# A convolution-and-attention kernel on one core: the second layer's matmuls in another order, and wide tiles for the relative logits' transposes

## The chip, the core and the metric

The kernel runs on one NeuronCore of a Trainium2 chip. The core has five engines that run side by side and meet at semaphores: TensorE (PE, matmuls and transposes; its weight loads are listed apart as PEld), VectorE (DVE), ScalarE (ACT), GpSimd (POOL) and SyncE (SP, which only issues DMAs here). The metric is the time of one execution on the device in microseconds. The kernel before the change took 2448.43 us, the median of three runs (2446.56 to 2452.04).

## The reference

Eight images of 32x32 pixels and 256 channels go through two layers, all in fp32. Cut to what matters:

```python
x = x + L0_conv(_gn(x), ...)                    # layer 0: 3x3 convolution (192 channels) beside
                                                # 8-head attention with relative logits (64 channels)
t = _to_tokens(x)                               # 1024 tokens an image
t = t + L1_attn(_ln_t(t), W_q, W_k, W_v, W_o, b_o)
t = t + L1_ffn(_ln_t(t), Wr, br, W1, b1, W2, b2, gamma, beta)   # two of eight experts an image

def L1_attn(inputs, W_q, W_k, W_v, W_o, b_o):   # U = 128
    Q, K, V = inputs @ W_q, inputs @ W_k, inputs @ W_v
    w = softmax(Q @ K.T / sqrt(U))
    return (w @ V) @ W_o + b_o + inputs

def L0_attention:                               # 8 heads of 8 channels
    logits = q @ k.T + rel_w + rel_h            # relative logits of row and column
    weights = softmax(logits)
```

The change lies in the second layer's attention (`L1_attn`) and in the work of the next image's first layer that is threaded through it.

## The kernel before, in words

One program handles the images one after the other, and then the expert layer for all of them. Within the loop over images the order of TensorE's instructions is the order in the text (`manual_schedule` for PE); the orders on VectorE, ScalarE and GpSimd are set by the framework's scheduler. So work of the next image is woven in by hand, as Python generators that are advanced a step at a time.

Image b goes through these stages:

- `conv_layer_attention` (L675 on): first-layer attention, in steps s. A step takes two score products of one head and 128 rows (`score`, L583) with a maximum on VectorE (L591), two groups of exponentials (`weigh`, L623 and L631) and their products with the values (`gather`, L640); the first 10 steps have scores alone. Products of the image's convolution that are still to do are spread over those 10 steps: `first` of them ahead of the first step, then `todo` in each.
- Near its end `ahead()` normalises the next image, and `more()` starts that image's `input_steps` (keys, queries, values).
- `attention_layer` (L758 on): layer norm, transposes of the normalised tokens (`tpn`, L779), query and key projections (`pq`, L795), value projection (`pv1`, L811), then a loop over eight tiles of 128 queries: `scores(i)` (L832, maximum L841, exponential L843), `turn(i)` (eight transposes of the weights, L852, copied out half by VectorE, L855, half by ScalarE, L857), and for every two tiles `gather(ib)` (sixteen products with the values, L863, copied out by ScalarE as `os`, L867) and `project(ib, os)` (output projection L875, then VectorE's additions L879 and statistics L880).
- Meanwhile `fill(us)` advances the next image's `input_steps`. Each step yields a length in us and a number of convolution products, which `fill` then runs (`conv.run`). The steps are: relative logits (`prel`, L468, 32-column products, copied out at L480 and L482), eight steps of them, then the transposes of the width logits (`tpw`, L493, copied into `rwq` at L495 and L497), four steps of four transposes. After the last, `Unit(0, ...)` is made, whose constructor issues the loads of the next image's first unit on SP (L555, L559, L566).

A convolution (`conv_steps`, L501 on) has 72 products (L515) in six groups of twelve; a group accumulates in one bank of PSUM and is copied out by ScalarE (L524), and GpSimd adds it to the image. The image's first 36 products run in `more` and `fill`, before its own turn, in the bank of the pool `po`, which is the only one; `conv.whole()` finishes an open group. The others run in the pool `st`.

The PSUM pools: `lg`, two tiles of two banks (scores, `prel`); `st`, three tiles of one bank (`tpn`, `tpw`, `pq`, `pv1`, `tp`, `pa1`); `po`, one tile of one bank. A tile asked for when none is free makes its first writer wait for the reader of an older one.

Of the kernel before, what the change touches and what calls it, by code (L numbers as in the profile page):

```python
# [20 lines left out]
NT = S // P  # L21
# [15 lines left out]
def kernel(  # L37
# [54 lines left out]
    with ExitStack() as ph:  # L92
# [27 lines left out]
        def st_tile(name):  # L120
            return ps_st.tile([P, 512], FP, tag="st", name=name)
# [263 lines left out]
        def input_steps(b, held):  # L385
# [69 lines left out]
            for which in range(2):  # L455
                for half in range(2):
                    prs = lg_tile("prel")
                    for i in range(16):
                        a = half * 16 + i
                        for g in range(NG):  # L460
                            rows = slice(DK + 32 * g, DK + 32 * g + 32)
                            dst = prs[:, g, i * 32 : (i + 1) * 32]
                            if which == 0:
                                table, mov, m = half_w, kqv[rows, :, a], WW - 1 - a
                            else:
                                table, mov, m = half_h, kqv[rows, a, :], HH - 1 - a
                            for k in range(2):
                                nc.tensor.matmul(  # L468
                                    dst[64 * k : 64 * k + 64], lhsT=table(rows, m, k), rhs=mov, start=True, stop=True
                                )  # L470
                        if i == 7:
                            yield 1.4, 4 - which * half
                    for g in range(NG):
                        if which == 0:
                            dst = rw[g].rearrange("p (x y) -> p y x", y=WW)[:, half * 16 : half * 16 + 16, :]
                            src = prs[:, g, :].rearrange("p (y x) -> p y x", x=HH)
                        else:
                            dst, src = rh[g][:, half * 512 : (half + 1) * 512], prs[:, g, :]
                        if g == 0:
                            nc.vector.tensor_copy(dst, src)  # L480
                        else:
                            nc.scalar.copy(dst, src)  # L482
                    if which == 0 and half == 1:
                        for g in range(NG):
                            nc.sync.dma_start(out=rwd[g], in_=rw[g])
                    yield 1.4, 4 - which * half

            for t2 in range(NT // 2):
                tp = st_tile("tpw").rearrange("p (t g c) -> p t g c", t=2, g=NG)
                for i in range(2):  # L490
                    t = t2 * 2 + i
                    for g in range(NG):
                        nc.tensor.transpose(tp[:, i, g, :], rw[g][:, t * P : (t + 1) * P], ident)  # L493
                if t2 % 2:
                    nc.vector.tensor_copy(rwq[:, t2 * 2 : t2 * 2 + 2], tp)  # L495
                else:
                    nc.scalar.copy(rwq[:, t2 * 2 : t2 * 2 + 2], tp)  # L497
                yield 0.43, 0
            held["units"] = [Unit(0, kq, rh, rwd)]

        def conv_steps(b, place):  # L501
# [179 lines left out]
        def conv_layer_attention(b, units, kq, rh, rwd, rwq, conv, early, ahead, more):  # L681
# [6 lines left out]
            units.append(Unit(1, kq, rh, rwd))  # L688
            left = conv.left
            lead = NT + LAG  # L690
            first = min(left, 3 * KC)
            conv.run(first)
            left -= first
            for s in range(NU * NT + lead + 2):
# [60 lines left out]
            more(0, 4)  # L755


        def attention_layer(b, fill, whole):  # L758

# [20 lines left out]
                for kc in range(KC):  # L782
                    nc.scalar.copy(nT[:, kc, q * 512 : (q + 1) * 512], tps[kc].rearrange("p j t -> p (j t)"))
            nc.gpsimd.tensor_tensor(T[b], T[b], bo.to_broadcast([P, NT, C]), ALU.add)
            fill(5.6)
            whole()

            qkv = f_tile("qkv").rearrange("p a e s -> p (a e s)")
            qk = [qkv[:, i * S : (i + 1) * S] for i in range(2)]
# [1 line left out]
            for i in range(2):  # L791
                for q in range(2):
# [10 lines left out]
                        nc.vector.tensor_copy(qk[i][:, q * 512 : (q + 1) * 512], pq)  # L803
                    else:
                        nc.scalar.copy(qk[i][:, q * 512 : (q + 1) * 512], pq)
            for q in range(2):
                pv = st_tile("pv1").rearrange("p (j u) -> p j u", u=U)
                for j in range(4):
                    t = q * 4 + j
# [70 lines left out]
                    nc.vector.bn_stats(st2[:, t, :], tt)  # L880
                    nc.vector.bn_aggr(mv2[:, b, t, :], st2[:, t : t + 1, :])

            for i in range(NT + 1):
                if i < NT:
                    scores(i)
                ib, odd = divmod(i - 3, NIB)
                os = None
                if ib >= 0 and not odd:
                    os = gather(ib)
                elif i:  # L890
                    fill(0.8)
                if i:
                    turn(i - 1)
                if os is not None:
                    project(ib, os)
            fill(1.0)
            for ib in range(max(0, (NT - 2) // NIB), NT // NIB):
                os = gather(ib)
                fill(0.8)
                project(ib, os)  # L900


            m = mv2[:, b]
# [33 lines left out]
        class Conv:  # L937
# [13 lines left out]
            def whole(self):  # L951

                self.run(self.left % (6 * KC))
# [17 lines left out]
        with tc.manual_schedule(engines={mybir.EngineType.PE}):  # L971
            conv = Conv(0)
            means = []
            for b in range(B):
# [36 lines left out]
                def fill(us):  # L1011

                    while us > 0:
                        took, products = next(steps, (None, None))
                        if took is None:
                            break
                        us -= took
                        conv.run(products)

                means.append((b, *attention_layer(b, fill, conv.whole)))  # L1020
                fill(1000.0)
                del T[b]
            token_mean(*means.pop())

# [282 lines left out]
```

## Time and profile before

| | |
|---|---|
| median of three runs | 2448.43 us |
| the profiled execution, its own time | 2444.67 us |
| its span, first to last instruction | 2442.9 us |
| mean granted TensorE clock | 0.981 |
| scores of the second layer (L832) | 119.1 us busy in 256 records |
| its value products (L863) | 116.6 us in 512 |
| convolution products (L515) | 236.1 us in 1152 |
| transposes `tpw` (L493) | 19.6 us in 128 |

A line of the profile names the source line, the engine, the operation, the tile written and the tile read, and their shapes. `x8` means that eight instructions in a row are merged. In brackets stands how long the engine had been idle and what it waited for. An image takes some 239 to 240 us, from one first score of its second layer to the next. The expert layer is the last 443 us of the span.

### The profile page before, as it was taken

To read this page: it belongs to the slowest core of one execution; us is meant where nothing else is said; L and a number is where in the kernel's file an instruction comes from. 1 tells how busy PE (TensorE), PEld (TensorE's weight loads), DVE (VectorE), ACT (ScalarE), POOL (GpSimd) and SP (SyncE) were. 2 spreads that over 40 slices of the span, in tenths; PEclk is the share of its full clock that TensorE was granted. 3 is DMA by queue.
4 is the path that set the end of the run, shared out by engine and by line. 5 is a ranking of instruction groups with operands and counts; after the bars stand their busy time and mean duration, and the time that the engine had idled before them with its cause. 6 is when DMAs were issued, how large, how long until landed. Compare 5 with 4: busy or idle time off the path is not lost. (4 is left out here: it accounts for less than half of the span.)

```text
span 2442.9 us, 41840 instructions
## 1 busy us (share of the span) xinstructions
PE 2314.1 (95%) x17273; PEld 1299.7 (53%) x17273; DVE 1485.5 (61%) x2661; ACT 1026.1 (42%) x1717; POOL 475.6 (19%) x446
## 2 busy tenths in 40 slices
PE   5999999999999999999999999999998879999998
PEld 4535643564366436643663376337632546666665
DVE  7776487548755875587467746774774434444443
ACT  2255336433643464346335732563266323222232
POOL 3202130213031202210230023002301032222221
PEclk7999999999999999999999999999999989999999
DMA  4521242134222412240324032403240032121210
GB/s 124 82 40 27 41 97 39 35 46 90 32 43 57 80 22 51 57 85 9 58 70 72 4 57 70 72 4 57 60 66 2 23 121 69 69 69 69 70 60 26
DMA packets 71468, 135.82 MB, mean 56 GB/s; under 512 B 12000, under 2 KB 24168, under 8 KB 69232
## 3 DMA queue, kind: packets, MB, share of 16 engines
q1 hardware_dynamic: 65488, 115.47, 23.7%
q0 software_dynamic: 3056, 15.73, 1.9%
q8 instruction: 136, 2.23, 0.4%
q10 hardware_dynamic: 2736, 1.97, 0.3%
q14 instruction: 52, 0.43, 0.1%
HBM read 53.43 MB, written 25.17 MB: 32 GB/s over the span
## 5 line engine op out<-in xcount | busy, mean ns | idle before, releaser
L591 DVE TENSOR_REDUCE my<-lg 128x32 f32<-128x1024 f32 x512 | 618.5, 1223 | 161.8 <-PE st L623 125.9
L631 ACT ACTIVATE PT<-st 128x512 f32<-128x512 f32 (+1 forms) x944 | 541.6, 633 | 306.2 <-PE st L623 301.7
L623 PE MATMUL st<-F,km 32*128 32x512 f32 x2048 | 545.2, 641 | 17.2 <-DMA F<-mb 11.9
L583 PE MATMUL lg<-km,F 24*128 24x512 f32 x2048 | 534.9, 637 | 6.1 <-DMA F<-kq 3.7
L640 PE MATMUL po<-PT,vall 128*32 128x256 f32 (+1 forms) x3200 | 315.1, 453 | 2.9 <-ACT PT L631 2.4
L583 PEld LDWEIGHTS lg<-km,F 24*128 24x128 f32 x2048 | 156.0, 183 | 186.5 <-issue 112.1
L515 PE MATMUL pc<-convw,gdif 128*128 128x192 f32 x1152 | 236.1, 345 | 11.5 <-ACT m L524 8.7
L640 PEld LDWEIGHTS po<-PT,vall 128*32 128x32 f32 x3200 | 66.9, 108 | 314.6 <-issue 280.1
L515 PEld LDWEIGHTS pc<-convw,gdif 128*128 128x128 f32 x1152 | 186.8, 192 | 81.5 <-issue 59.9
L623 PEld LDWEIGHTS st<-F,km 32*128 32x128 f32 x2048 | 177.5, 184 | 96.3 <-issue 43.5
L1220 PE MATMUL phd<-n2T,w 128*128 128x512 f32 x512 | 223.7, 594 | 0.0
L1237 PE MATMUL py<-w,hT 128*128 128x256 f32 x1024 | 223.6, 379 | 0.0
L1237 PEld LDWEIGHTS py<-w,hT 128*128 128x128 f32 x1024 | 194.6, 190 | 33.3 <-issue 7.4
L311 POOL TENSOR_TENSOR T<-T,l0b 128x2048 f32<-128x2048 f32 x8 | 36.4, 4546 | 633.5 <-PE tpx L304 633.5
L1220 PEld LDWEIGHTS phd<-n2T,w 128*128 128x128 f32 x512 | 97.0, 191 | 114.9 <-issue 107.7
L1244 DVE TENSOR_TENSOR r<-py,n 128x256 f32<-128x256 f32 x64 | 27.1, 423 | 215.0 <-PE py L1237 215.0
L863 PE MATMUL po<-pt,qkv 128*128 128x256 f32 x512 | 116.6, 381 | 11.3 <-DVE pt L855 11.3
L524 ACT COPY m<-pc 128x384 f32<-128x384 f32 x48 | 23.0, 479 | 247.3 <-PE pc L515 247.3
L1227 ACT ACTIVATE hT<-phd,b1c 128x512 f32<-128x512 f32 x128 | 86.3, 686 | 96.5 <-PE phd L1220 96.3
L841 DVE TENSOR_REDUCE nm<-lg 128x1 f32<-128x1024 f32 x64 | 78.1, 1220 | 77.5 <-PE lg L832 77.5
L780 POOL TENSOR_TENSOR T<-T,n 128x256 f32<-128x256 f32 x64 | 47.1, 743 | 372.8 <-DVE n L775 372.8
L832 PE MATMUL lg<-qkv 128*128 128x512 f32 x256 | 119.1, 593 | 0.0
(250 smaller groups left out, 2627.6 us busy)
## 6 DMA issues: line engine op xcount, KB each, us to landing
F<-rh SPq DMA_DIRECT2D x256, 128.0 KB
F<-kq SPq DMA_DIRECT2D x256, 64.0 KB
F<-rwd SPq DMA_DIRECT2D x256, 64.0 KB
w<-in_L_ffn_W_dram SPq DMA_DIRECT2D x32, 512.0 KB
rwd<-rw SPq DMA_DIRECT2D x16, 512.0 KB
Td<-T POOLq DMA_DIRECT2D x8, 1024.0 KB, 8.3
T<-Td SPq DMA_DIRECT2D x8, 1024.0 KB
out_dram<-yo SPq DMA_DIRECT2D x16, 512.0 KB
```

Source lines behind the costliest of these rows:

```text
L515: nc.tensor.matmul(pc[:, v, :], lhsT=gflat[:, 2 * pair + v, kc, at : at + P], rhs=convw[:, 2 * pair + v, dy, kc * CO : (kc + 1) * CO], sta ...
L583: nc.tensor.matmul(lg[:, a, :], lhsT=self.F[r : r + 24, a, 0, i * P : (i + 1) * P], rhs=KM[self.g][r : r + 24, a].rearrange("p e k -> p (e ...
L591: nc.vector.tensor_reduce(my[:, :, hl], lg.rearrange("p a (y x) -> p y a x", y=WW), AX.XY, ALU.max)
L623: nc.tensor.matmul(st[:, i, :] if len(heads) > 1 else st, lhsT=KM[self.g][r : r + 32, a, e, :], rhs=self.F[r : r + 32, a, e, :], start=Tru ...
L631: nc.scalar.activation(self.pts[j][:, hs, :], st, AF.Exp)
L640: nc.tensor.matmul(self.po[32 * hl : 32 * hl + 32, cols], lhsT=vall[:, j, h * (DH + 1) : h * (DH + 1) + 32], rhs=self.pts[j][:, hl, cols], ...
L832: nc.tensor.matmul(lg[:, h, :], lhsT=qk[0][:, i * P : (i + 1) * P], rhs=qk[1][:, h * 512 : (h + 1) * 512], start=True, stop=True,)
L841: nc.vector.tensor_reduce(nm, lg, AX.X, ALU.max, negate=True)
L863: nc.tensor.matmul(po[:, 0:IB], lhsT=v1[:, jc, :], rhs=pt[:, jc, :], start=jc == 0, stop=jc == NT - 1)
L1220: nc.tensor.matmul(phd, lhsT=ws[k][0][:, kc, f * P : (f + 1) * P], rhs=n2T[:, kc, q * 512 : (q + 1) * 512], start=kc == 0, stop=kc == KC - 1,)
L1227: nc.scalar.activation(hT[:, k * NF + f, :], phd, AF.Gelu, bias=b1c[:, f, k * B + b : k * B + b + 1])
L1237: nc.tensor.matmul(py, lhsT=hT[:, k * NF + f, j * P : (j + 1) * P], rhs=ws[k][1][:, f, :], start=k == 0 and f == 0, stop=k == TOPK - 1 and ...
```

## The change

Five things are changed, all in the order of work or in the tiles used; the arithmetic is the same.

```diff
@@ input_steps: products per step, and wide transposes
-                            yield 1.4, 4 - which * half
+                            yield 1.4, 4 - (which == half == 0)
...
-                    yield 1.4, 4 - which * half
+                    yield 1.4, 4 - (which == half == 0)
-            for t2 in range(NT // 2):
-                tp = st_tile("tpw").rearrange("p (t g c) -> p t g c", t=2, g=NG)
-                for i in range(2):
-                    t = t2 * 2 + i
+            for t4 in range(2):
+                tp = lg_tile("tpw").rearrange("p q (t g c) -> p (q t) g c", t=2, g=NG)
+                for i in range(4):
+                    t = t4 * 4 + i
                     for g in range(NG):
                         nc.tensor.transpose(tp[:, i, g, :], rw[g][:, t * P : (t + 1) * P], ident)
...
-                yield 0.43, 0
+                yield 0.86, 0
@@ conv_layer_attention
-            first = min(left, 3 * KC)
+            first = left % (3 * lead)
@@ attention_layer (now given the Conv object, not its method whole)
-            fill(5.6)
-            whole()
+            fill(1000.0)
+            conv.whole()
...
-            for q in range(2):
+
+            def values(q):
                 pv = st_tile("pv1").rearrange("p (j u) -> p j u", u=U)
...
-            for i in range(NT + 1):
-                if i < NT:
-                    scores(i)
+            for i in range(NT):
+                scores(i)
+                if i < 2:
+                    values(i)
                 ib, odd = divmod(i - 3, NIB)
-                os = None
                 if ib >= 0 and not odd:
                     os = gather(ib)
-                elif i:
-                    fill(0.8)
                 if i:
                     turn(i - 1)
-                if os is not None:
+                if ib >= 0 and not odd and i + 1 < NT:
                     project(ib, os)
-            fill(1.0)
-            for ib in range(max(0, (NT - 2) // NIB), NT // NIB):
-                os = gather(ib)
-                fill(0.8)
-                project(ib, os)
+            turn(NT - 1)
+            project(NT // NIB - 2, os)
+            os = gather(NT // NIB - 1)
+            conv.place[0] = st_tile
+            conv.run(2)
+            project(NT // NIB - 1, os)
@@ the loop over images
-                means.append((b, *attention_layer(b, fill, conv.whole)))
-                fill(1000.0)
+                means.append((b, *attention_layer(b, fill, conv)))
```

- The value projection, sixteen products, ran as a block behind the query and key projections. Now its first half stands behind the scores of tile 0 and its second half behind those of tile 1.
- The end of the layer ran as: gather 2, transposes of tile 6, projection 2, transposes of tile 7, gather 3, projection 3. Now it is: gather 2, transposes of tile 6, transposes of tile 7, projection 2, gather 3, two convolution products of the next image (in an `st` bank), projection 3.
- The convolution products of the eight steps of relative logits were 4, 4, 4, 4, 4, 4, 3, 3, and are 3, 3, 4, 4, 4, 4, 4, 4. The sum stays 30; with 4 in `more` and 2 in the step ahead it is 36.
- `first`, the products ahead of an image's first scores, was 6, and is what is left over when 30 is taken out: 4 of 34 for all images but the first (30 then go in tens of three), and 12 of 72 for the first (then six a step, where it had six steps of seven and four of six).
- The transposes of the width logits go eight to a `lg` tile of two banks, in two steps, where they went four to an `st` tile of one bank, in four; so there are two copies of 1024 elements (one on ScalarE, one on VectorE) for four of 512.

## The prediction

> **What bounds the kernel now.** I read the page first: TensorE (PE) is busy 95% of the span, no other engine more than 61%.
>
> ```profile
> span 2442.9 us, 41840 instructions
> PE 2314.1 (95%) x17273; PEld 1299.7 (53%) x17273; DVE 1485.5 (61%) x2661; ACT 1026.1 (42%) x1717; POOL 475.6 (19%) x446
> ```
>
> An average can hide stages with another limit, so next the stretches of one image (the second; columns: length, then busy time of each engine, granted clock, DMA share, GB/s).
>
> ```profile
> 454.00:494.00 40.00, 37.17 (x685) 31.54 (x684) 15.92 (x39) 12.45 (x22) 17.10 (x18) 1.00 0.36 67
> 508.00:541.00 33.00, 30.98 (x150) 23.09 (x151) 19.78 (x44) 14.67 (x27) 0.00 (x0) 1.00 0.02 5
> 548.00:579.00 31.00, 30.51 (x154) 16.16 (x150) 28.51 (x38) 3.12 (x7) 19.98 (x25) 1.00 0.44 107
> ```
>
> The first two, which the change rewrites, are PE's: VectorE is under 60% busy, ScalarE under 45%. The third, the first scores of the next image, is VectorE's (28.51 of 31). A microsecond saved on PE ahead of it counts only if VectorE can start earlier too.
>
> Third, the list of waits on PE alone: who was waited for, us in total, times, longest.
>
> ```profile
> PE po L863 <- DVE pt L855: 11.3, 8, 1.4
> PE pc L515 <- ACT m L524: 8.7, 14, 0.6
> PE tp L852 <- ACT pr L843: 8.6, 8, 1.1
> ...
> PE tpw L493 <- ACT rwq L497: 4.7, 7, 0.7
> PE pa L875 <- ACT os L867: 4.1, 8, 0.5
> PE tpw L493 <- ACT nT L783: 4.0, 7, 0.6
> ```
>
> Six rows, 41.4 us, each 7, 8 or 14 times: they fall once or twice in every image. Last, the timeline of the same image, where I measure from start to start, since the end of a matmul is modelled.
>
> ```profile
> 471.71 0.92 PE L515 MATMUL pc<-convw,gdif 128*128 128x192 f32 x4 [0.62 <-ACT m L524]
> ...
> 491.12 0.66 PE L493 MATMUL tpw<-ident,rw 128*128 128x128 f32 x4 [0.68 <-ACT rwq L497]
> ...
> 508.60 1.09 PE L852 MATMUL tp<-ident,pr 128*128 128x128 f32 x8 [1.08 <-ACT pr L843]
> ...
> 540.49 3.72 PE L863 MATMUL po<-pt,qkv 128*128 128x256 f32 x16 [1.41 <-DVE pt L855]
> ...
> 544.73 1.13 PE L875 MATMUL pa<-wo,os 128*128 128x256 f32 x4 [0.52 <-ACT os L867]
> ```
>
> [...] PE stands still for each row above. [...] Here the granted clock was 0.50 from 61 to 70 us and 0.99 from 70 to 74[...].
>
> **The change part by part.** The instruction counts of PE stay; what goes is waiting. Two records are one fp32 product, one record a transpose.
>
> *Values between the first scores.* Before: the eight score matmul records of two tiles start at 503.93. Four of them take 1.71 us where nothing waits (519.04 to 520.75), so the transposes could start at 507.35; they start at 508.60: 1.25 us lost. Tile 0's softmax needs 4.67 us from the start of its scores (503.93 to 508.60). Afterwards 2x1.71 of scores and 3.57 of values (500.36 to 503.93) lie there, 6.99 us: covered, with 2.3 to spare. Gain 1.25x8 = 10.0. The two ScalarE copies of the values (0.58 each) now queue among exponentials, on an engine with over half its time free: nothing. One cover goes: scores start at 500.36, their second half at about 501.22, and the last copy of the keys ends at 501.14. I take 0, with up to 0.6 an image (another copy ahead of it), 4.8, in the range.
>
> *Last projection but one behind the last transposes.* Eight transposes take 0.88 (520.75 to 521.63); the last begin at 538.04, so the gather could start at 538.92, and starts at 540.49: 1.57 lost. VectorE is why: its copy (539.78) stands behind project's two additions and two statistics. Afterwards the transposes come 0.87 earlier, their copies go ahead of those additions, and the projection (0.87) lies over them. The second transpose group may wait some 0.1 for a third st bank. Gain 1.47x8 = 11.8.
>
> *Two products before the last projection.* A gather takes 3.45 (523.35 to 526.80), so the projection could start at 543.94; it starts at 544.73: 0.79 lost to the copy of os. Two products are 4 records at 0.172 (8 in 1.41), 0.69: 0.1 stays. They come out of the six that open the next image (now four), so nothing is added. Not for the last image. Gain 0.69x7 = 4.8. Does VectorE profit? Its first maximum started at 548.94 after waiting 0.58 for PE. The next scores come 2.3 us earlier; VectorE's own chain behind the projection (0.88+0.74+0.30+0.20) then ends some 3.3 us after that projection's start at 543.15 on the old clock, at 546.4, and the scores are there at 546.6. It just does.
>
> *Wide transposes.* Before: transposes at 489.84, 491.12 (0.85 lost of 1.28), 492.56 (0.74 lost of 0.95): 1.59 an image, both for an st bank. In two lg tiles the first is free since the copies of rh at 484.8 and the second since 490.0; nothing waits. Copies: two of 0.585 on ScalarE become one of 1024 elements, about 1.04 by the row of equal width (exponentials, 1036 ns); two of 0.690 on VectorE become one of 1.22 (the row of xT, 1221 ns). The wide ScalarE copy stands ahead of the two copies of nT, which then end at 493.3 on a clock where their reader is due at 493.8: hidden, by 0.5. Gain 1.59x7 = 11.1.
>
> *Products 3,3,4,...,4 instead of 4,...,3,3.* With 4+2 ahead the groups of twelve now end at the end of a step. Before, two groups ended inside one and the next product waited for the copy out of the only po bank: 470.17 to 471.71 is 1.54 for 0.69 of work, 0.85 lost, 14 times. Now a transpose pair (0.2) and 64 prel records (1.15) lie between, against about 0.75 for the copy. At the first group ScalarE may take the copy of rw (1.05) ahead; then 0.4 stays. I take half of that. Gain 11.9-1.4 = 10.5.
>
> *First image.* Its last wide transposes need a bank whose copies end at 54.8 (ScalarE), so the first product moves from 53.0 to about 56.4. But twelve products instead of six now stand before the first scores, where PE waited 3.65 us for DMA[...], and six later steps have one product less (0.35 each). Between a loss of 3 and a gain of 6; I take +3.
>
> *Calls with one answer.* The rest of the fill steps, called at the layer's end before and ahead of its query-key projections now, had run out there anyway: the next image's first unit issues its last loads at 493.50, beside the first projection. So the SP queue keeps its order. The second unit's loads (from 539.14, behind the last transposes) come 0.87 us earlier on that clock, and are wanted eight steps, some 25 us, later. GpSimd gets the same adds; nothing on PE waits for it there.
>
> Sum: 10.0+11.8+4.8+11.1+10.5+3.0 = 51.2. The profiled execution took 2444.67 (span 2442.9), 3.8 below the median of 2448.43. From the first: 2393.5; from the median: 2397.2. I predict 2397.
>
> **Rivals.**
> - *Half of it comes back as new waits*: ScalarE and VectorE orders are not written out by hand, and the wide copy, the key copy and the rw copy each stand within 0.5 us of their reader. Losing the fill stage's 21.6 and 0.6 an image leaves 51.2-26.4 = 24.8: about 2423; with half of the fill stage, 2412. Against: those engines are half idle there.
> - *The end of the layer is absorbed*: the stage behind it is VectorE's, so the 1.47+0.69 might move nothing for seven images: 15.1 back, 2412. For: VectorE's 0.2 us of margin. Against: its wait of 0.58 at 548.94.
> - *Slower: the clock.* [...] 0.981 on average now. Over 2314 us of PE work 0.1 point costs 2.4 us, so 51 us are gone at about 0.960; at 0.950 it is 2397+73, some 2470. Against: from 2000 to 2443 us PE is busy 435.57 of 443 at a clock of 1.00.
> - *It doesn't do what it says*: a wait of the six rows is only shifted to the neighbour, and the time stays within 5 us of 2448.
>
> **How the numbers follow.** Forecast 0.74 (own range 2388 to 2408: no residue and the best first image, 2391, against the key wait and the worst first image, 2408, with 3 us of scatter). Half comes back 0.12; absorbed 0.07; nothing 0.02; slower 0.05. Range 2387 to 2416 holds the first, the third and part of the second, some 8 in 10. What can be told from no change here is 0.2%, 5 us. Faster 0.93, same 0.02, slower 0.05.
>
> **What would show it.** Right: the six rows gone from PE's waits; from the first query-key projection to the end of the last projection some 3.5 us shorter an image; pq starting 3.3 us earlier behind the first transposes of tpn; VectorE's first maximum still waiting for PE. Wrong: new PE rows against rw, nT or qkv; a clock below 0.97; an image period (now 239 to 240 us) shorter by less than 5 us. If period and waits both fall but the time doesn't, the loss lies in the first image or behind the last.

## The result, and the profile after

The change makes the kernel 1.6% faster: 2409.18 us, the median of five runs (2407.99 to 2409.86), against 2451.59 for the kernel before beside it (five runs, 2446.56 to 2452.09). The ratio is 0.9836, with a 95% interval of 0.9824 to 0.9849, so some 42 us. The profiled executions took 2407.99 and 2444.67 us: 36.7 us less where the working had promised 51.2. The question is where the other 14.5 went.

The head of the page after the change, in the same columns as before:

```profile
span 2406.2 us, 41836 instructions
PE 2317.1 (96%) x17273; PEld 1308.3 (54%) x17273; DVE 1481.2 (62%) x2653; ACT 1022.7 (43%) x1709; POOL 475.7 (20%) x446
```

The same 17273 matmul records are busy for 3.0 us *longer* than before (2317.1 for 2314.1). If nothing had happened but waits going away, this number would have stayed. The mean granted TensorE clock says the same: 0.974 for 0.981.

TensorE's list of waits (who was waited for; us in total, times, longest):

```profile
PE lg L583 <- DVE my L591: 4.8, 20, 0.4
...
PE tpw L493 <- ACT rwq L497: 1.1, 1, 1.1
...
PE pa L876 <- ACT os L868: 0.8, 1, 0.8
PE pc L515 <- ACT convw L280: 0.7, 1, 0.7
```

Of the six rows shown before, 41.4 us in 7, 8 or 14 pieces each, four are gone. Two are left with one piece each: the wide transposes of the first image, and the last projection of the last image, which has no products of a next image to lie under. In the timeline of the second image the five places shown before now run without a wait:

```profile
463.97 1.57 PE L515 MATMUL pc<-convw,gdif 128*128 128x192 f32 x8
...
480.71 1.04 PE L493 MATMUL tpw<-ident,rw 128*128 128x128 f32 x8
...
495.54 1.04 PE L853 MATMUL tp<-ident,pr 128*128 128x128 f32 x8
...
525.92 3.62 PE L864 MATMUL po<-pt,qkv 128*128 128x256 f32 x16
...
530.06 1.13 PE L876 MATMUL pa<-wo,os 128*128 128x256 f32 x4
```

No bracket follows any of them. But one row has come up: the first-layer scores `lg` now wait for VectorE's maximum (L591) 4.8 us in 20 pieces, which was 1.2 us before. So I cut the second image into three stretches by its own events rather than by round times: from its first query-key product of the next image's first layer to the first projection `pq`; from there to the next image's first score; and the steps that have scores alone. The columns are length, then the busy time of each engine with its instructions, granted clock, DMA share, GB/s. The kernel before:

```profile
453.18:493.49 40.31, 37.48 (x688) 31.75 (x686) 16.23 (x40) 12.91 (x24) 16.59 (x18) 1.00 0.35 65
493.49:547.74 54.25, 51.24 (x239) 36.19 (x237) 25.48 (x56) 19.67 (x34) 1.41 (x3) 1.00 0.23 34
547.74:579.29 31.55, 30.77 (x155) 16.42 (x154) 28.93 (x39) 3.50 (x7) 20.43 (x26) 1.00 0.44 107
```

The changed kernel:

```profile
444.63:481.58 36.95, 36.59 (x687) 31.86 (x685) 16.73 (x44) 11.96 (x21) 15.17 (x17) 1.00 0.35 68
481.58:532.42 50.84, 50.84 (x239) 36.31 (x237) 25.47 (x53) 20.21 (x36) 2.34 (x2) 1.00 0.24 35
532.42:566.86 34.44, 33.46 (x158) 17.97 (x157) 29.10 (x43) 3.56 (x7) 21.04 (x26) 0.90 0.44 104
```

In the second stretch TensorE is busy for all of its 50.84 us: there is nothing left to win there but work itself. The two stretches are 3.4 us shorter each. The third, in which the change touches nothing (both kernels run thirty convolution products in it), is 2.8 us longer, and its clock is 0.90. (By its own event it ends at 566.77; the line shown runs on for 0.09 us and three records.)

The same three stretches of all seven images that a next one follows, and what lies around them, in us (profiled executions):

| stretch | before, each | after, each | sum of the change | predicted |
|---|---|---|---|---|
| start, and the first image up to its fill stage | 214.0 | 213.4 | -0.6 | -3 |
| fill stage: query-key product to first `pq` | 40.3 | 36.9 to 37.0 | -23.5 | -21.6 |
| second layer: `pq` to the next first score | 54.2 | 50.8 to 51.0 | -23.7 | -23.9 |
| steps with scores alone | 31.5 to 31.6 | 32.0 to 34.4 | +13.5 | 0 |
| rest of the first layer | 111.4 to 123.9 | 111.4 to 123.9 | 0.0 | 0 |
| last image's second layer, experts | 550.6 | 548.2 | -2.4 | -2.7 |
| sum | | | -36.7 | -51.2 |

The gain came where it was put and nearly to the size that was put on it. It was given back in one stage behind it. Its seven lengths after the change are 32.0, 34.4, 32.0, 34.2, 33.3, 34.2 and 34.4: two at 32.0, the others above. A *fall* is from here on a stretch in which the granted clock is 0.50. The granted clock in stretches of 2 us, from 3.6 us behind the first score of the second image on, shows what sets them apart:

```profile
536.00:538.00 2.00, 1.75 (x9) 0.90 (x8) 1.84 (x3) 0.00 (x0) 1.82 (x4) 1.00 0.91 291
538.00:540.00 2.00, 2.00 (x9) 1.28 (x11) 1.48 (x3) 0.48 (x1) 1.82 (x3) 0.50 0.65 221
540.00:542.00 2.00, 2.00 (x10) 0.78 (x3) 0.67 (x1) 0.00 (x0) 1.82 (x3) 0.50 0.54 102
542.00:544.00 2.00, 2.00 (x9) 1.56 (x12) 1.69 (x2) 0.00 (x0) 1.82 (x3) 0.50 0.54 76
544.00:546.00 2.00, 2.00 (x12) 0.92 (x9) 0.71 (x1) 0.00 (x0) 1.82 (x3) 0.79 0.54 66
```

From 538.00 to 544.83 the clock is halved, although TensorE had stood still for no more than 0.25 us of the 2 before. In the timeline around the fall (start, length; in brackets the idle time before and who ended it):

```profile
532.42 1.14 PE L583 MATMUL lg<-km,F 24*128 24x512 f32 x8
533.49 1.24 PE L515 MATMUL pc<-convw,gdif 128*128 128x192 f32 x6
534.90 1.20 PE L583 MATMUL lg<-km,F 24*128 24x512 f32 x4 [0.17 <-DVE my L591]
536.35 1.20 PE L583 MATMUL lg<-km,F 24*128 24x512 f32 x4 [0.25 <-DVE my L591]
537.47 1.80 PE L515 MATMUL pc<-convw,gdif 128*128 128x192 f32 x6
...
533.62 1.23 DVE L591 TENSOR_REDUCE my<-lg 128x32 f32<-128x1024 f32 x1 [0.42 <-PE lg L583]
534.76 0.19 DVE L907 RECIPROCAL mv<-mv 128x8 f32<-128x8 f32 x1
534.99 0.17 DVE L909 TENSOR_TENSOR mr<-mv 128x8 f32<-128x8 f32 x1
535.07 2.35 DVE L591 TENSOR_REDUCE my<-lg 128x32 f32<-128x1024 f32 x2
...
541.33 2.36 DVE L591 TENSOR_REDUCE my<-lg 128x32 f32<-128x1024 f32 x2 [1.78 <-PE lg L583]
```

From some 534.55 (six records of products after 533.49, at 0.172 to 0.18 a record) to 537.47 TensorE does scores alone, and each of these records has 24 active rows (`24*128`); those of the convolution have 128 (`128*128`). The first eight, two calls of `score`, were issued in 1.07 us (532.42 to 533.49); the next eight stand in two fours, 1.45 apart, because each call waits for the tile that a maximum of 1.23 us sets free. Behind the fall the score products are late, and VectorE, which has the stage's bound, waits 1.78 us for them. Two things can be read off here. The reciprocal of the second layer's statistics (L907) now stands between the first two maxima, beside L909, which stood there before; so the second maximum starts 2.65 us behind the first score and not 2.42, and TensorE, which waited the 0.17 us before as well, waits another 0.25. And something lowers the clock. The experiments are about the second.

The stage's extra 13.5 us divide as follows: images without a fall take 32.0 where they took 31.5 to 31.6, some 0.45 each, 3.1 in all; the five with falls have 10.4 on top, 1.3 for a fall of 3.4 us and 2.2 to 2.4 for one of 6.8. Three of these falls start 5.5 to 5.6 us behind the first score (6.1 of the 10.4 us), two start 24 us behind it (4.4).

### The profile page after: what moved, and what is told of

Same layout as the page of the kernel before. It is cut to its first block, busy times and chain, and to the rows that moved or that the text cites. A ratio compares the mean times of both kernels' runs of the same rounds, so it can differ in the third digit from the quotient of the medians.

```text
span 2406.2 us, 41836 instructions
## 1 busy us (share of the span) xinstructions
PE 2317.1 (96%) x17273; PEld 1308.3 (54%) x17273; DVE 1481.2 (62%) x2653; ACT 1022.7 (43%) x1709; POOL 475.7 (20%) x446
## 5 line engine op out<-in xcount | busy, mean ns | idle before, releaser
L591 DVE TENSOR_REDUCE my<-lg 128x32 f32<-128x1024 f32 x512 | 617.9, 1223 | 170.4 <-PE st L623 125.9
L515 PEld LDWEIGHTS pc<-convw,gdif 128*128 128x128 f32 x1152 | 192.5, 197 | 72.4 <-issue 65.2
L524 ACT COPY m<-pc 128x384 f32<-128x384 f32 x48 | 23.7, 493 | 238.9 <-PE pc L515 217.5
```

Of the source, the lines that this page charges most:

```text
L515: nc.tensor.matmul(pc[:, v, :], lhsT=gflat[:, 2 * pair + v, kc, at : at + P], rhs=convw[:, 2 * pair + v, dy, kc * CO : (kc + 1) * CO], sta ...
L591: nc.vector.tensor_reduce(my[:, :, hl], lg.rearrange("p a (y x) -> p y a x", y=WW), AX.XY, ALU.max)
```

## The experiments

All edits are against the changed kernel if not said otherwise. Two theories stood against each other. *Thin work*: the clock falls where the matmuls use few rows, whatever TensorE's busy time is; six products ahead of the first score (as before the change) or convolution products near the scores should keep it up. *Dense work*, the slower rival of the prediction: the clock falls because TensorE has fewer pauses. The change put two of the six products that opened the stage under the last projection (`conv.run(2)`), which leaves four ahead of the first score.

**The changed kernel once more, and six products first.**

> The changed kernel itself, as the yardstick of the three runs beside it: some 42 us under the kernel before. Both theories expect the granted TensorE clock to fall to 0.5 again in the first-layer score steps of most images (six of seven in its profile).

It took 2408.2 us, median of five (2404.03 to 2411.12), 0.9839 of the kernel before [0.982, 0.9858]. Its profiled execution has the scores-only stage at 32.0, 33.6, 32.0, 34.4, 32.0, 34.1 and 34.3: falls again, in other images (in this stage four of seven, where the first profile has five, and not the six of the expectation). So which images fall isn't set by the kernel's text alone.

```diff
-            conv.place[0] = st_tile
-            conv.run(2)
             project(NT // NIB - 1, os)
```

> The changed kernel with the two products taken out of the layer's end and put back in front of the next image's scores (six there). Theory A (the clock falls because a stretch of the score steps without convolution products got too thin: PE reaches the scores before VectorE has finished the statistics): the layer's end is 0.7 us longer, VectorE's statistics are done before its first maximum, the clock stays at 1.00 in the score steps, which take 31.5 us again instead of 32.0 to 34.4; in all some 8 us faster than the changed kernel. Theory B (the clock falls because matmuls are denser than before): the layer is still denser than before, so the falls stay, and the kernel is 4 to 5 us slower than the changed one.

Without the two products, `left % 30` gives six ahead of the first score again. 2401.6 us on the same chip (2398.28 to 2407.28), 0.9811 [0.9791, 0.9831]: leaving out a part of the change that gains seems to make the kernel faster, though the two intervals still overlap (0.982 and 0.9831). The stage of the second image in its profile:

```profile
535.13:566.70 31.57, 30.80 (x157) 16.43 (x156) 28.95 (x39) 3.51 (x7) 20.47 (x26) 1.00 0.47 111
```

and its opening:

```profile
535.13 1.14 PE L583 MATMUL lg<-km,F 24*128 24x512 f32 x8
536.20 1.24 PE L515 MATMUL pc<-convw,gdif 128*128 128x192 f32 x6
537.61 2.40 PE L583 MATMUL lg<-km,F 24*128 24x512 f32 x8 [0.17 <-DVE my L591]
539.94 1.24 PE L515 MATMUL pc<-convw,gdif 128*128 128x192 f32 x6
```

All seven stages are 31.5 to 31.6, with a clock of 1.00. The layer ahead is 51.5 instead of 50.84, 0.65 an image longer, as the prediction's 0.69 for the two products says. The stretch of scores alone is shorter by 0.23 (537.26 to 539.94, 2.69, against 2.92), since the reciprocal of VectorE's statistics is done before the first maximum starts. One image has a fall of 10.2 us elsewhere, 33.4 us behind the first score, just behind this stage; it costs 4.6 us.

**Convolution products between the two score calls of a step.**

```diff
                     units[u].score(2 * j, rwq)
...
+                    if not weigh:
+                        part = -(-left // (lead - s)) // 2
+                        conv.run(part)
+                        left -= part
                     units[u].score(2 * j + 1, rwq)
...
-                    todo = -(-left // (lead - s))
+                    todo = -(-(left + part) // (lead - s)) - part
```

> The changed kernel with the three convolution products of a score step set one between its two heads and two behind them, so that no stretch between convolution products is longer than about half a step. Theory A (too thin a stretch): the clock stays at 1.00 in the score steps, stage 31.5 to 32.0 us, 10 to 13 us faster than the changed kernel. Theory B (too dense): the falls stay, within 2 us of the changed kernel or slower.

If thin stretches are the trouble, halving them should have helped. It took 2490.49 us, median of six: five between 2488.89 and 2501.33 (mean clock 0.954 to 0.961), one at 2444.76 (0.979). The profile is of one of the five. Even the sixth is 36.6 us above the changed kernel's 2408.2, and the timeline of a step at a clock of 1.00 shows where that comes from:

```profile
590.23 1.13 PE L583 MATMUL lg<-km,F 24*128 24x512 f32 x4
591.29 0.59 PE L515 MATMUL pc<-convw,gdif 128*128 128x192 f32 x2
591.81 1.13 PE L583 MATMUL lg<-km,F 24*128 24x512 f32 x4
592.87 0.92 PE L515 MATMUL pc<-convw,gdif 128*128 128x192 f32 x4
```

One call's four records take 1.06 us from start to start (590.23 to 591.29). In the changed kernel the eight records of both calls took 1.07. Line 583 puts the four products of these calls in four different groups of 32 rows. In the changed kernel's trace their first four records start within 0.02 us of one another (532.418 to 532.438, each given 0.69 us there), the next four 0.53 us behind; so the four run side by side. With other products between the calls, the two of one call take as long as the four do together. A step is longer by what that costs; the stage became 36.5 in the five images without a fall, 4.5 more than in the changed kernel, and 46.2 in two. The first image's score steps took 84.2 us instead of 43.0, with one fall of 75.1 us. That one may well be what sets the five slower executions apart, but the sixth has no profile. Two stretches of the first image:

```profile
80.00:90.00 10.00, 10.00 (x24) 4.74 (x22) 2.45 (x2) 1.13 (x3) 3.08 (x4) 0.50 0.60 101
110.00:120.00 10.00, 10.00 (x25) 4.87 (x22) 3.29 (x5) 0.48 (x1) 3.08 (x4) 0.50 0.00 0
```

TensorE is busy without a gap (as far as modelled ends can tell) and its clock stays at half. So a share of busy time alone isn't what lowers it here. As a cure the edit failed: four score records took the time of eight. Between the theories it doesn't decide alone, since dense work fell here too. But the second layer, busy 50.84 of 50.84 us at 1.00, is just as dense and doesn't fall; thin work fits both.

**The first step made thinner.**

```diff
-            first = left % (3 * lead)
+            first = left % (3 * lead) + (3 if b else 0)
...
-                    todo = -(-left // (lead - s))
+                    todo = 0 if b and s == 0 else -(-left // (lead - s))
```

> The changed kernel with the three products of the first score step run ahead of it (seven before the first scores, none in the first step, three in each later one), so that a stretch of some 5 us has scores alone. Theory A: the clock falls there in all seven images and longer, some 5 to 10 us slower than the changed kernel. Theory B: the density is the same over the stage, so the falls come as often as in the changed kernel, within 2 us of it.

The three products of the first step run ahead of it, so that two steps of scores stand together. 2414.79 us, 0.9873 [0.9852, 0.9895], 6.6 more than the changed kernel beside it. The moved products make the layer ahead 1.0 us longer (51.8). The stage took 36.1, 34.4, 31.6, 34.4, 31.5, 31.6 and 36.1: the falls come 2.9 to 3.6 us behind the first score, 2 us earlier than in the changed kernel, as the thin stretch does, and last up to 10.2 us. But four images fell and not all seven. The thin stretch was there in each, so it wasn't enough; something else goes in too.

**What the falls have in common: one grid.** The falls of a profile start and end on one grid. In the changed kernel's trace the 25 changes of the granted clock, over 2386 us, lie within 0.001 us of a grid with a step of 3.4133 us; so do the 17 in the trace of the kernel before, over 2423 us. Four falls start at 538.00, 1022.70, 1490.32 and 1705.36 us; the differences are 142, 137 and 63 times 3.4133. Their lengths are 6.8 us, those of the other three between 200 and 1840 us 3.4. A *window* is from here on a stretch of 3.41 us between two neighbouring points of this grid. The image's period, 231.2 to 234.1 us from one first score to the next, is 67.7 to 68.6 windows, so each image meets the grid at another phase. For each image I took the time from its first score to the window's end that lies around 5.4 us later:

| kernels | falls at 5 us behind the first score | no such fall |
|---|---|---|
| four products ahead (changed kernel twice, and the four below that undo another part) | window ends at 5.0 to 5.82 us: 17 of 42 images | up to 4.78, from 5.87 on |
| six ahead (kernel before, six products first twice, and the two below that start from six) | 5.17 to 5.55 us: 6 of 35 | up to 4.88, from 5.70 on |

Every window that ended in the interval fell, and none outside it. A window of 3.41 us that ends 5.0 to 5.82 us behind the first score holds the stretch of scores alone of the changed kernel (2.13 to 5.05 us) or nearly so. How thin is thin? I counted, in every window that ends in this stage, from 1.6 us behind its first score on, the time of products of 128 rows (from the starts of the records, at most 0.18 us each, 0.215 for the spare ones below; the small `pmt` and `pmx` left out), in all fourteen profiles. The 37 windows that end in a fall hold at most 0.69 us of it. Of 814 others (windows within a fall left out), 803 hold 0.70 or more, and eleven hold 0.60 to 0.68. TensorE's idle time doesn't sort them: it is 0.00 to 1.34 us in the windows with a fall, and 0.00 to 1.34 in the others. With products between the calls the opening holds 0.97 and more in every window, and none fell there. With six ahead the stretch is 0.23 us shorter and the interval narrower. The grid is taken from the falls; that the clock follows what lies in these windows is not shown, only that the counts go with the falls.

The same count answers for the falls at 24 us, which the six profiles of the first row have in 7 of 42 images (window ends at 23.52 to 24.04, and no other window ended there) and those of the second in none. In the changed kernel the products at 19.5 and 23.4 us behind the first score start 3.83 us apart, in images that have not fallen before; with six ahead it is 3.57. The seven windows hold 0.60 to 0.69 us of products; with six ahead none there holds less than 0.85.

**Eight products ahead.**

```diff
-            first = left % (3 * lead)
+            first = left % (3 * lead) + (2 if b else 0)
```

> The changed kernel with its two products in the layer's end kept and six, not four, ahead of the next scores. The layer is then as long as with the two products undone (51.5 us), but the wait for the copy of os is filled. If the stage behind it is bound by VectorE's chain from that projection, which both kernels start at the same time, it takes 31.5 us with no or one fall, and the kernel is within 3 us of the one with six products first (some 2402). If the two products themselves bring the falls (PE denser, theory B), they stay in about half of the images, and it is 8 us or more above that.

Here the opening is fuller, and the last two steps of the stage are left with two products each instead of three (564.63 and 568.02 in the second image, 0.92 us of four records, 3.4 us apart). 2435.36 us, median of six, 0.9947 [0.9928, 0.9967]: nearly the whole gain of the change is lost. Falls came 33 to 36 us behind the first score in six of seven images, in windows that begin at the end of the last thinned step's products or behind it and so hold none of them; the changed kernel has no falls there. They are three and four windows long; the rest of the first layer took 112.8 to 117.2 instead of 111.4. The number of products is the same, only spread otherwise, and the falls moved to where they are missing. Neither result of the expectation came: 2435 is far from 2402, and the loss lies in a place that neither branch named. At 5 us four images fell, which the expectation gave to dense work; but all four windows ended at 5.17 to 5.55, the interval in which the kernel with the spare pair (below), without the two products under the projection, falls as well. So an opening with six products isn't immune, it only has the narrower interval. (The two under the last projection are kept here, so eight are ahead in all.)

**Spare products to fill the thin stretches.** Both put products whose results nobody reads where the matmuls use few rows.

```diff
                     conv.run(todo)
                     left -= todo
+                if b and s < 4:
+                    nc.tensor.matmul(st_tile("warm")[:, 0:C], lhsT=wqkv1[:, 0, 0, :], rhs=wo, start=True, stop=True)
```

> The changed kernel with one extra full-array product (128x128 by 128x256, its result unused, about 0.43 us) behind the convolution products of each of the first four score steps, all images but the first; order otherwise as it is. Theory A (the clock falls for want of full-array work): no fall in the score steps, stage at 32.0 us in all images, some 10 us faster than the changed kernel though PE does 12 us more. Theory B (too dense): the falls stay or become more, same time or slower.

2402.68 us, 0.9816 [0.98, 0.9832]. One fall in seven images, at 25 us, behind the reach of the spare products; and none in the one image whose window ended between 5.0 and 5.82 (at 5.45). In the other six no window ended there, so this is one case. The median is some 6 us under the changed kernel's 2409.18 and 2408.2, where 10 were expected; the intervals overlap (from 0.982 on there, up to 0.9832 here). The spare products themselves lengthen the stage: 32.5 to 33.1 in the images without a fall, against 32.0. In the profiles its seven lengths sum to 232.6, against 234.4 and 232.4 in the changed kernel's two.

The second starts from the kernel with six products first:

```diff
+                if s == NU * NT + 5 and b + 1 < B:
+                    spare = lg_tile("warm")
+                    for i in range(2):
+                        nc.tensor.matmul(spare[:, 0, i * C : i * C + C], lhsT=wqkv1[:, 0, 0, :], rhs=wo, start=True, stop=True)
```

> The kernel with six products ahead of the first scores, and two extra full-array products (0.86 us) in every image where PE stands still for ScalarE's two table loads near the end of the first-layer attention. Theory A: the falls there (113 us and more instead of 111.4 in four of six images) go, 5 to 10 us faster than that kernel, some 2395. Theory B: no gain, 6 us slower if nothing hides the products.

This is for a fall that both kernels have, in the last steps of the first-layer attention, about 133 us behind the first score (one to three images of seven; 112.9 to 113.1 instead of 111.4). In the trace of the kernel before, two table loads of ScalarE stand there, 1.28 us each (from 676.41 and 677.93), and TensorE waits 0.75 us for the exponentials behind them. Such falls follow windows that end 11.00 to 11.24 us ahead of the next image's first query-key product. Of the images with a spare pair only the one that took 118.6 (with another fall before) had such a window, at 11.01, and it fell. The pair ran there ahead of the window, from 15.5 to some 14.4. The other images show nothing either way. What the run does show is the price: the pair costs 1.0 us in each image (112.4 to 112.5 instead of 111.4), and the time is 2408.21 us, 0.9835 [0.9821, 0.9849], 6.6 to 8 us slower than without. That is the time expected of dense work, but seven pairs of 1.0 us account for it; that spare products can remove the fall at the end is not shown.

**The parts undone one by one**, a single execution each, read from the profile by stretches.

```diff
-            def values(q):
+            for q in range(2):
...
-                if i < 2:
-                    values(i)
```

> The changed kernel with the value projection as a block behind the query and key projections again. By the prediction's step the wait of PE before the first transposes returns: from the first projection to the next image's first scores 52.1 us instead of 50.8 (1.25 more), the other stages as they are.

`pq` to first score: 52.0 to 52.2 instead of 50.8 to 51.0, 1.2 an image (1.25 predicted). Time 2412.04.

```diff
-                if ib >= 0 and not odd and i + 1 < NT:
+                if ib >= 0 and not odd:
                     project(ib, os)
             turn(NT - 1)
-            project(NT // NIB - 2, os)
```

> The changed kernel with the last projection but one ahead of the last transposes again. By the prediction's step the wait before the last gather returns: 52.3 us instead of 50.8 (1.47 more), the other stages as they are. VectorE and ScalarE do the same work in both.

`pq` to first score: 52.4, 1.54 an image (1.47 predicted). Time 2418.24.

```diff
-            for t4 in range(2):
-                tp = lg_tile("tpw").rearrange("p q (t g c) -> p (q t) g c", t=2, g=NG)
-                for i in range(4):
-                    t = t4 * 4 + i
+            for t4 in range(NT // 2):
+                tp = st_tile("tpw").rearrange("p (t g c) -> p t g c", t=2, g=NG)
+                for i in range(2):
+                    t = t4 * 2 + i
...
-                yield 0.86, 0
+                yield 0.43, 0
```

> The changed kernel with the width logits' transposes four to a one-bank tile again. By the prediction's step the two waits for a bank return: from the first key-query product of an image to the second layer's projections 38.5 us instead of 36.95 (1.59 more). The score steps of the next image are those of the changed kernel: theory A expects falls of the clock in about half of the images there, and 32.0 us where it does not fall.

Fill stage 38.6 to 38.7 instead of 36.9 to 37.0, 1.69 an image (1.59 predicted). Time 2415.03.

```diff
-                            yield 1.4, 4 - (which == half == 0)
+                            yield 1.4, 4 - which * half
...
-                    yield 1.4, 4 - (which == half == 0)
+                    yield 1.4, 4 - which * half
```

> The changed kernel with convolution products 4,4,4,4,4,4,3,3 again. By the prediction's step the two waits for the only po bank return: 38.65 us instead of 36.95 in the same stage (1.70 more). The score steps as in the changed kernel: falls in about half of the images.

38.6, 1.67 an image (1.70 before the allowance of 0.2). Time 2414.07. The four parts gain what they were said to, each by itself, and none of them hides another. The times alone don't show it: 2412.04 with 1.2 an image lost is only 2.9 over the changed kernel's median of 2409.18, because the number of falls differs from one execution to the next.

**Six products first, again.**

> The kernel with six products first once more, beside the one with eight, and as a second sample of where the clock falls: theory A expects none or one fall in the score steps of seven images, and some 2402 us, 6 to 8 under the changed kernel.

2400.07 us (2397.95 to 2401.96), on another chip, 0.9799 [0.9783, 0.9816]. Again no fall in seven stages (31.5 to 31.6). Over two runs it is the fastest of all the kernels here, 6.6 us under the changed kernel in the run that had both on one chip.

One thing was still to be settled: in the two profiles of this kernel no window happened to end between 4.84 and 5.70, so that none of them shows whether it would have fallen, and the kernel with the spare pair, which opens its stage in the same way, fell twice of seven. Is the better time luck? In part the two profiles are. But each execution has its mean granted clock on record. It was 0.980 over 31 executions of the kernel before (0.977 to 0.984), 0.974 over ten of the changed kernel (0.972 to 0.978), 0.980 over ten with six products first (0.978 to 0.983). The mean clock doesn't settle it alone: the four kernels that undo another part also have four products ahead, and their single executions stand at 0.977 to 0.980. The stage does better. Its seven lengths sum to 230.3 to 234.4 us in all six profiles with four ahead, to 220.8 or 220.9 in three with six, and to 225.6 with the spare pair, falls included.

## Why the prediction was right, and where its sum was too large

The forecast of a gain of some 2% was right in direction and mechanism; 2409 lies 12 us above the predicted 2397, within the range of 2387 to 2416 but outside the likeliest case's own 2388 to 2408. By its steps:

- *Values between the first scores*, 1.25 an image: 1.2 when undone. Right, and the feared wait for the last key copy isn't among the waits.
- *Last projection but one behind the last transposes*, 1.47: 1.54 when undone. Right.
- *Two products before the last projection*, 0.69: 0.65 in the layer. The term is right and its balance wrong. That "nothing is added" because the two come out of the six that open the next image is the sentence that failed. While the six ran, VectorE ended its reciprocal ahead of the first maximum; with four it does not. That adds 0.45 an image, and it makes two stretches of scores alone 0.23 and 0.26 us longer; with four ahead 24 of 42 images fell in this stage, with six 6 of 35. Without this part of the change the kernel was 6.6 us faster on the same chip.
- *"It just does"*, on VectorE's margin of 0.2 us at the first maximum: there it does. The first maximum starts 1.20 us behind the first score in both kernels, and waits for TensorE. The sum stopped one instruction too early. In the kernel before, the reciprocal came ahead of that maximum:

```profile
548.15 0.20 DVE L907 RECIPROCAL mv<-mv 128x8 f32<-128x8 f32 x1 [0.28 <-ACT mv L906]
...
548.94 1.23 DVE L591 TENSOR_REDUCE my<-lg 128x32 f32<-128x1024 f32 x1 [0.58 <-PE lg L583]
```

  Now it comes behind it, and TensorE waits for the second (0.17 and 0.25 in the timeline above, 4.8 us over the kernel). 3.1 us in seven images; the absorbed end of the layer, a rival at 7%, is true to a fifth of its 15.1.
- *Wide transposes* and *products 3, 3, 4, ...*: 1.59 and 1.5 predicted, 1.69 and 1.67 when undone. The 0.2 kept back for a copy of `rw` wasn't needed. Together they gained 23.5 where 21.6 was put.
- *First image*, +3, my estimate between a loss of 3 and a gain of 6: 0.6. The bank wait was shorter than feared (1.10 us, and the first product started at 53.13 and not at 56.4), but the clock under the twelve products, 0.64 from 56 to 57 us and 1.00 from 57 on, didn't last:

```profile
50.47 1.97 PE L493 MATMUL tpw<-ident,rw 128*128 128x128 f32 x8 [1.10 <-ACT rwq L497]
...
53.13 5.92 PE L515 MATMUL pc<-convw,gdif 128*128 128x192 f32 x24 [0.69 <-ACT convw L280]
...
62.64 3.27 PE L583 MATMUL lg<-km,F 24*128 24x512 f32 x6 [2.54 <-DMA F<-kq]
```

  After the products TensorE waits 2.54 us for the loads of its first unit, and from 64 to 66 us the clock is at 0.50 again; the steps with one product less gain about 0.15 each where 0.35 was put.
- *The clock*, named as the way to a slower kernel: the effect came, but not in the second layer, which kept 1.00 (busy 50.84 us of 50.84). What fell was the clock of the thin stage behind them, and with it the kernel's mean, from 0.981 to 0.974. The changed kernel's profile has 37.5 us of falls between 200 and 1840 us, the one before 6.8: 30.7 more at a clock of 0.50, all of it in that stage. That is 15 us of matmul time by an estimate from the first image before the change, where fourteen records of convolution products took 4.78 us from start to start at 0.50 (from 65.29 us) and 2.47 at 1.00 (from 71.14). The stage grew by only 10.4 on their account. Why not by 15 was not shown; my reading is that part of the slower matmuls lies under VectorE's work, 29.10 of 34.44 us in the second image.

The size that was missing is thus the stage with scores alone, which the prediction put at nothing: 3.1 us of VectorE and 10.4 of clock, 13.5 of the 14.5; the rest is the first image's 2.4, less 1.9 that the fill stage gained over its estimate, and small ends. One of the prediction's own signs says the same. The image's period was 238.0 us on average (237.4 to 239.2, not 239 to 240) and is 233.1, shorter by 4.95, where less than 5 was named as a sign of being wrong. That the time still lies in the range owes something to the range, which was wide enough for rivals that did not come.

Is the wider interval enough to explain how often the kernels fall? An estimate: if the phases were spread evenly over the 3.41 us, the intervals with four ahead (0.82 to 1.09 us at 5, 0.52 to 1.20 at 24, from the outermost falls and the nearest windows without one) would catch 39 to 67% of the images, and that with six ahead (0.38 to 0.82) 11 to 24%. Measured are 24 of 42, 57%, and 6 of 35, 17%.

Three things stay open. Why the products at 19.5 and 23.4 us lie further apart with four ahead isn't known; one addition on VectorE (L595) takes 0.91 us there in place of 0.28, at the same time as additions on GpSimd. The falls behind this stage, at 33 us and near the end of the first layer, lie among other matmuls, which the count above doesn't cover. And all thin work here is the same kind of product, so whether its 24 rows, its missing neighbours or something else about it goes with the falls was not varied.

## What to carry to other kernels

When waits ahead of a stage are removed, look at what the first microseconds of that stage did: work that opens it may be giving another engine the time to finish, and moving it forward into a gap can make the narrow matmuls behind it stand alone for longer (here 2.92 us for 2.69), at the price of the clock (here down to 0.50 in 24 of 42 images, for 6 of 35). Price each edit in the stretch between two events of the kernel and not by the whole time, which here moved by as much with the alignment to the grid of the falls as with an edit of 1 us an image. Keep matmuls of different row groups next to one another (here eight records in 1.07 us, against four in 1.06 where others stood between).

## What the runs showed of the hardware

- The granted clock didn't follow TensorE's busy time: 10.00 of 10.00 us busy at a clock of 0.50 (products between the score calls), and a fall with 0.25 us of pauses in the 2 us before it. In the stage with scores alone, what went with the falls was a window of 3.41 us with at most 0.69 us of matmuls of 128 rows, the rest of it matmuls of 24 rows of 128 and short waits.
- The falls that end within the traces of the kernel before and of the changed one last multiples of 3.413 us, 3.4 to 27.3. From 200 us on to the last image, those of the other runs are 3.4, 6.8 or 10.2 us, once 13.7 (eight products ahead); the run with products between the score calls has 23.9 in two places and 75.1 in its first image. Where VectorE has the bound, a fall costs 0.3 to 0.4 of its length (1.3 for 3.4, 2.2 to 2.4 for 6.8).
- Score products in four row groups take 1.07 us for eight records; in two row groups, four records take 1.06. Other products between the two calls of a step cost the overlap.
